# Two tiles of output rows projected one batch later, and the last tile's halves in two PSUM tiles

## The chip, the core and the metric

The kernel runs on one core of a Trainium2 chip. The metric is the device time of one execution in microseconds; the median of several executions is given. A profiled execution has a span, from the first to the last instruction of the core, and a time of its own, which is a little longer.

## The reference

The program is a cross attention over 16 batches. Every batch has 100 query rows of 640 elements, and a context of 722 rows of 384 elements, the last 4 of which are handled apart.

```python
enc = ctx[:, :718];  ca = ctx[:, 718:]
hs  = mha(x @ Wq, enc @ Wk, enc @ Wv)              # 8 heads of 80
q1  = einsum('btc,th->bch', ca, Wq_ca)[:, indices]  # 100 of 384 rows
h1  = mha(q1, x, x)
hs2 = mha(h1 @ Wq, ca @ Wk_ca, ca @ Wv_ca)          # 4 keys
out = (hs + hs2) @ Wout + b_out + x
```

All is float32. The change touches only the last line: `out` has 1600 rows (16 batches of 100), and they are made in tiles of up to 128 rows that don't stop at the borders of batches.

## The kernel before

**Loop.** After a start that loads and rearranges weights, one Python loop (L1102) writes out 16 iterations, one for each batch `b`. The order of the instructions on every engine is the order in which the code issues them. An iteration `b` runs, on TensorE, in this order:

1. `scores` (L604, tile `s_ps`) of batch `b` against its keys, three groups;
2. `softmax2` (L792, `z_ps`) and `products` (L730, `y_ps`), parts of the small attention;
3. `last.transpose()` (L907, `hst_ps`): the attention output of batch `b - 1` is transposed, and ScalarE copies it into tiles `hsT` of 128 output rows each;
4. the values of batch `b` and the keys of batch `b + 1`, interleaved (`vv.go`, `kk.go`; L425 and L456, tiles `v_ps*` and `k_ps*`), then `last_keys` (L549, `kT_ps`);
5. `last.project()` (L932, `o_ps`): every output tile that became complete with batch `b - 1` is multiplied with `Wout`. This is 5 chunks times 2 column halves, 10 matmuls, each two passes with a weight load each in the trace;
6. in odd iterations, `queries` (L525, `q_ps`) for the next two batches;
7. the attention product `a_ps` (L1283) of batch `b`, 96 small matmuls.

Beside it, VectorE and ScalarE make the softmax, GpSimd the small attention's elementwise work (`scores1`, L765; `values2`, L854) and the sums of the context (`enc_sums`, L491), and loads for batch `b + 2` are issued near step 5: `enc`, `mb`, `rest`, `ca` and every other time `xT` from the sync engine's queue (SP), `vb` (1 MB) from GpSimd's.

**Output tiles.** `OC` (L33) lists the row tiles: eleven of 128 rows, one of 64 (rows 1408 to 1471) and the last of 128. A tile is complete with the batch that holds its last row: batches 1, 2, 3, 5, 6, 7, 8, 10, 11, 12, 14, 14 and 15. It is projected in the iteration after. So iterations 1, 5, 10 and 14 project no tile. The 64 rows go through `project_few` in iteration 15, the last tile after the loop.

**Class `Last`** (L873) does this for one batch. `load` (L881) loads the rows of `x` for the tile into `xn` from SP, and GpSimd adds the bias (L892). `project` (L925) takes a `pair`, a PSUM tile of two banks, one bank for each column half; there are two such pairs, shared with the scores and the values. VectorE adds `xn` (L951), and SP stores it (L952). `xn` and `hsT` have two buffers each. For the last batch (`split`) the addition and the store are made for each half apart (L945, L948), and the matmuls come in three calls: chunk 0 of both halves, chunk 1 of both halves, then chunks 2 to 4 of the first half and chunks 2 to 4 of the second.

Of the kernel before, what the change touches and what calls it, by code (L numbers as in the profile page):

```python
# [10 lines left out]
ALU = mybir.AluOpType  # L11
# [3 lines left out]
B, S, H = 16, 100, 640  # L15
# [15 lines left out]


OC = [(r, P) for r in range(0, B * S - P - 64, P)] + [(B * S - P - 64, 64), (B * S - P, P)]  # L33
HT = NH * T

QC = [(0, 64), (64, S)]
# [10 lines left out]
for h in range(NH):  # L47
    lo = h * D
    while lo < (h + 1) * D:
# [3 lines left out]
        lo = hi  # L53
# [71 lines left out]
def kernel(  # L125
# [18 lines left out]
    nc = tc.nc  # L144
# [14 lines left out]
    def pair(name):  # L159
        tile = ps2.tile([P, 2, 512], F32, tag="ps2", name=name)  # L160
        return tile

    def bank(name):
        return pair(name)[:, 0]
# [21 lines left out]
    def hs_tile(name):  # L186
        return main.tile([P, H], F32, tag="hs", name=name)

    def hsT_tile(name):
        return main.tile([P, HC, P], F32, tag="hsT", name=name, bufs=2)  # L190

    def xn_tile(name):
        return main.tile([P, H], F32, tag="xn", name=name, bufs=2)
# [120 lines left out]

    m2 = const.tile([P, HC, NG, HT], F32, name="m2")
    nc.gpsimd.memset(m2, 0.0)
# [8 lines left out]
    for c in range(HC):  # L325
# [13 lines left out]

    m_sb = [t[:, : B * HT] for t in (hs_tile("m_0"), xn_tile("m_1"), xn_tile("m_2"))]  # L340
    m_sb += [
        hsT_tile(f"m_{c}").rearrange("p c s -> p (c s)")[:, : B * HT] for c in range(3, HC)
    ]
    m_d = dram.tile([HC, P, B * HT], F32, name="m_d")

# [7 lines left out]
    for j in range(2):  # L353
        y = const.tile([S, NH, HT + 1], F32, name=f"y_{j}")
        nc.gpsimd.memset(y[:, :, HT:], 1.0)
        ys.append(y)
# [352 lines left out]
    class Second:  # L709
# [98 lines left out]
        def load(self):  # L808
            b = self.b
            self.vb = vb = vb_tile(f"vb_{b}")  # L810
            nc.gpsimd.dma_start(
                out=vb[:S],
                in_=va_d[b * T : (b + 1) * T, :].unsqueeze(0).to_broadcast([S, T, H]),
            )
# [58 lines left out]
    class Last:  # L873
# [7 lines left out]
        def load(self):  # L881

            self.xn = {}
            for r, (lo, n) in enumerate(OC):
                if not self.b * S < lo + n <= (self.b + 1) * S:
                    continue
                xn = self.xn[r] = spare[1] if r == len(OC) - 1 else xn_tile(f"xn_{r}")
                rows = x.rearrange("b s n -> (b s) n")[lo : lo + n]
                for at, cols in self.parts(n):
                    to = xn[at : at + n, : cols.stop - cols.start]  # L890
                    nc.sync.dma_start(out=to, in_=rows[:, cols])
                    nc.gpsimd.tensor_tensor(to, to, bias[at : at + n, cols], ALU.add)  # L892
# [7 lines left out]
        def transpose(self, chunks=[(0, HC)]):  # L900
# [4 lines left out]
            for c0, c1 in chunks:  # L905
                for c in range(c0, c1):
                    nc.tensor.transpose(  # L907
                        t_v[:, c], hs[:S, c * P : (c + 1) * P], ident[:S, :S]
                    )
                for r, (lo, n) in enumerate(OC):  # L910
                    first, end = max(lo, b * S), min(lo + n, (b + 1) * S)
                    if first >= end:
                        continue
                    if r not in hsTs:
                        hsTs[r] = (
                            spare[0].rearrange("p (c s) -> p c s", c=HC)
                            if r == len(OC) - 1
                            else hsT_tile(f"hsT_{r}")
# [6 lines left out]
        def project(self, chunks=range(HC)):  # L925
            for r, xn in self.xn.items():
                lo, n = OC[r]
                if chunks[0] == 0:
                    self.o_ps = pair(f"o_ps_{r}")
                o_ps = self.o_ps  # L930
                for c, k in [(c, k) for k in range(2) for c in chunks]:
                    nc.tensor.matmul(  # L932
                        o_ps[:n, k, : H // 2],
                        hsTs[r][:, c, :n],
                        wout_sb[:, c, k * (H // 2) : (k + 1) * (H // 2)],
                        start=(c == 0),
                        stop=(c == HC - 1),
                    )
                if chunks[-1] < HC - 1:
                    continue  # L940
                o_v = out.rearrange("b s n -> (b s) n")[lo : lo + n]
                if self.split:
                    for k in range(2):
                        cols = slice(k * (H // 2), (k + 1) * (H // 2))
                        nc.vector.tensor_tensor(  # L945
                            xn[:n, cols], o_ps[:n, k, : H // 2], xn[:n, cols], ALU.add
                        )
                        nc.sync.dma_start(out=o_v[:, cols], in_=xn[:n, cols])  # L948
                    continue
                both = xn[:n].rearrange("p (k d) -> p k d", k=2)  # L950
                nc.vector.tensor_tensor(both, o_ps[:n, :, : H // 2], both, ALU.add)  # L951
                nc.sync.dma_start(out=o_v, in_=xn[:n])  # L952

        def project_few(self, r):
            lo, n = OC[r]
            xn = self.xn.pop(r)
            o_ps = psumk(f"o_ps_{r}")
            for c in range(HC):
                for at, cols in self.parts(n):
                    nc.tensor.matmul(  # L960
                        o_ps[at : at + n, : H // 2],
                        hsTs[r][:, c, :n],
                        wout_sb[:, c, cols],
                        start=(c == 0),
                        stop=(c == HC - 1),
                    )
            nc.vector.tensor_tensor(
                xn[:, : H // 2], o_ps[:, : H // 2], xn[:, : H // 2], ALU.add
            )
            o_v = out.rearrange("b s n -> (b s) n")[lo : lo + n]  # L970
            for at, cols in self.parts(n):
                nc.sync.dma_start(out=o_v[:, cols], in_=xn[at : at + n, : H // 2])
# [26 lines left out]
    for n, heads in enumerate(HEADS):  # L999
        cols = len(heads) * B * T  # L1000
# [101 lines left out]
    for b in range(B):  # L1102
# [171 lines left out]
        for g in range(2):  # L1274
# [20 lines left out]
            cols = slice(4 * g * D, 4 * (g + 1) * D)  # L1295
# [66 lines left out]
```

## Time and profile before

| what | value |
|---|---|
| median of 3 executions | 960.67 us (958.2 to 962.56) |
| profiled execution, its own time | 961.78 us |
| its span | 960.1 us |
| mean granted TensorE clock | 0.992 of full |
| one projection of a tile on TensorE (`o_ps` start to next start) | 5.38 us |
| one set of queries (`q_ps` start to `a_ps` start) | 8.55 us |
| one addition of 128 x 640 (L951) | 0.82 us |
| one addition of 128 x 320 (L945) | 0.48 to 0.49 us |
| one bias addition of 128 x 640 (L892) | 1.55 us |

The two rows on the projection and the queries are differences of start times in the timeline of iteration 9 (609.17, 614.55 and 623.10 us). Since the matmuls of one step follow each other without a gap, a difference of starts is what the step costs. In this profile PE stands for TensorE's matmuls and PEld for its weight loads, which overlap; DVE is VectorE, ACT ScalarE, POOL GpSimd and SP the sync engine. A `q` after an engine's name is its instruction sequencer or its DMA queue.

### The profile page before, as it was taken

What the parts mean: (1) busy time and instruction counts of PE and PEld (TensorE: products, weight loads), DVE (VectorE), ACT (ScalarE), POOL (GpSimd) and SP (SyncE); (2) the same over time, 40 slices, a digit from 0 to 9 for tenths busy, and PEclk for the clock granted to TensorE, in tenths of its full rate; (3) what the DMA queues carried; (4) which work ended last, traced back from release to release, by engine and by line L of the source; (5) the groups of instructions that cost most, each with busy time, mean ns of one, the idle gap of its engine ahead of it and who ended that gap; (6) DMA issues with size and microseconds to landing.
All of it is one profiled execution on the core that took longest, in us unless ns stands there. A gap on an engine that the chain in (4) does not pass through costs nothing.

```text
span 960.1 us, 25609 instructions
## 1 busy us (share of the span) xinstructions
PE 942.0 (98%) x11215; PEld 801.9 (84%) x11215; DVE 674.0 (70%) x1083; ACT 361.8 (38%) x598; POOL 620.1 (65%) x570
## 2 busy tenths in 40 slices
PE   9899989999999999999999999999999999999998
PEld 6797869888798798978889787898879879898866
DVE  1647686695937869496874959559694796928883
ACT  1233433434324443342434334243432444314341
POOL 4646888485955768487663958638595476845713
PEclk9999999999999999999999999999999999999999
DMA  8912105021040301204040040401204031120100
GB/s 259 293 55 69 34 17 161 3 72 58 4 146 2 94 23 51 87 1 129 1 139 12 1 129 1 135 3 44 72 1 149 2 93 37 44 86 1 59 8 29
DMA packets 45255, 62.48 MB, mean 65 GB/s; under 512 B 13336, under 2 KB 37208, under 8 KB 43544
## 3 DMA queue, kind: packets, MB, share of 16 engines
q1 hardware_dynamic: 41608, 42.97, 15.1%
q0 software_dynamic: 2512, 16.72, 6.0%
q8 instruction: 88, 1.44, 0.6%
q10 hardware_dynamic: 1024, 1.15, 0.4%
q14 instruction: 23, 0.19, 0.1%
HBM read 55.26 MB, written 5.57 MB: 63 GB/s over the span
## 4 chain that ended last, share of the span: by engine, by line
PE 91%; DMA 3%; POOL 2%; DVE 1%; issue 1%; SPq 0%; ACT 0%; ACTq 0%; DVEq 0%; POOLq 0%
PE s_ps L604 11%; PE a_ps L1283 11%; PE v_psA L425 10%; PE v_psB L425 8%; PE k_psA L456 7%; PE kT_ps L549 7%; PE q_ps L525 7%; PE o_ps L932 7%; PE k_psB L456 6%; PE v_psC L425 3%; PE k_psC L456 2%; PE v_psE L425 2%; PE v_psD L425 2%; PE y_ps L730 2%; PE k_psE L456 1%; DMA wout_sb<-in_wqt 1%
## 5 line engine op out<-in xcount | busy, mean ns | idle before, releaser
L765 POOL TENSOR_TENSOR e<-ca,g 100x800 f32<-100x800 f32 x64 | 99.3, 1561 | 142.4 <-DVE most L1136 127.9
L854 POOL TENSOR_TENSOR hs<-vb,p 100x640 f32<-100x640 f32 x64 | 105.7, 1660 | 46.7 <-DVE p L840 38.8
L861 POOL TENSOR_TENSOR hs<-hs,hs 100x640 f32<-100x640 f32 x48 | 113.8, 2372 | 3.8
L1283 PEld LDWEIGHTS a_ps<-vs,st 120*64 120x64 f32 (+3 forms) x3072 | 109.0, 125 | 5.6 <-issue 5.2
L1283 PE MATMUL a_ps<-vs,st 120*64 120x81 f32 (+3 forms) x3072 | 112.0, 234 | 0.0
L425 PE MATMUL v_psA<-wv_sb,enc 128*120 128x320 f32 x360 | 112.0, 434 | 0.0
L1124 DVE TENSOR_TENSOR st<-st,over 120x1600 f32<-120x1600 f32 x48 | 106.9, 2229 | 0.0
L491 POOL TENSOR_TENSOR enc<-enc 128x240 f32<-128x240 f32 x135 | 101.1, 763 | 7.1
L604 PE MATMUL s_ps<-qp,kT 32*120 32x100 f32 x3072 | 99.5, 265 | 1.5 <-issue 1.5
L604 PEld LDWEIGHTS s_ps<-qp,kT 32*120 32x120 f32 x3072 | 96.7, 181 | 3.2 <-issue 1.8
L621 ACT COPY st<-s_ps 120x800 f32<-120x800 f32 x64 | 49.7, 829 | 127.3 <-PE s_ps L604 127.3
L425 PE MATMUL v_psB<-wv_sb,enc 128*120 128x320 f32 x300 | 93.1, 433 | 0.0
L772 POOL TENSOR_TENSOR e<-e,e 100x800 f32<-100x800 f32 x48 | 90.5, 1886 | 3.8
L456 PE MATMUL k_psA<-enc,wk_sb 128*128 128x240 f32 x360 | 88.4, 369 | 4.4 <-POOL enc L491 2.3
L456 PEld LDWEIGHTS k_psA<-enc,wk_sb 128*128 128x128 f32 x360 | 68.4, 191 | 21.9 <-POOL enc L491 2.8
L1294 DVE RECIPROCAL rs<-a_ps 100x4 f32<-100x4 f32 x32 | 5.8, 181 | 114.9 <-PE a_ps L1283 114.9
L425 PEld LDWEIGHTS v_psA<-wv_sb,enc 128*120 128x120 f32 x360 | 64.5, 183 | 23.0 <-issue 0.5
L1132 ACT ACTIVATE st<-st 120x1600 f32<-120x1600 f32 x48 | 73.9, 1539 | 22.5 <-DVE st L1124 22.5
L1136 DVE TENSOR_TENSOR most<-most,st 120x800 f32<-120x800 f32 x64 | 66.0, 1031 | 22.4 <-ACT st L615 21.2
L491 POOL TENSOR_TENSOR enc<-enc,rest 128x240 f32<-128x240 f32 x45 | 31.8, 706 | 74.2 <-DMA rest<-in_enct 27.4
L456 PE MATMUL k_psB<-enc,wk_sb 128*128 128x240 f32 x300 | 74.7, 372 | 0.0
L425 PEld LDWEIGHTS v_psB<-wv_sb,enc 128*120 128x120 f32 x300 | 54.8, 183 | 22.1 <-DVE vs L396 0.4
(137 smaller groups left out, 1764.9 us busy)
## 6 DMA issues: line engine op xcount, KB each, us to landing
vb<-va_d POOLq DMA_DIRECT2D x16, 1000.0 KB, 7.4
enc<-in_enct SPq DMA_DIRECT2D x30, 240.0 KB
enc<-in_enct SPq DMA_DIRECT2D x15, 360.0 KB
xT<-in_xt SPq DMA_DIRECT2D x8, 500.0 KB
rest<-in_enct SPq DMA_DIRECT2D x31, 120.0 KB
xn<-in_x SPq DMA_DIRECT2D x11, 320.0 KB
out<-xn SPq DMA_DIRECT2D x11, 320.0 KB
ca<-in_cas SPq DMA_DIRECT2D x16, 156.2 KB
```

Source lines behind the costliest of these rows:

```text
L425: nc.tensor.matmul(at[0][j][:KN, : H // 2], a_form(self.enc, f)[:, j * KN : (j + 1) * KN], wv_sb[:, W_AT[f]], start=first, stop=last, skip ...
L456: nc.tensor.matmul(at[:, i * KT : (i + 1) * KT], wk_sb[:, W_AT[f], i], a_form(self.enc, f), start=(first and i == 0), stop=last, skip_grou ...
L491: nc.gpsimd.tensor_tensor(out, left, right, op)
L525: nc.tensor.matmul(q_ps[:, : 2 * S].rearrange("p (j s) -> p j s", j=2), wq_sb[:, c, n * P : (n + 1) * P], xT[:, :, c, :], start=(c == 0), ...
L604: nc.tensor.matmul(s_ps[r][:n, 256 * a + lo : 256 * a + hi], kT[rows, c, u, j * KN : (j + 1) * KN], rhs, start=(a == 0 and c == 0), stop=( ...
L765: first = nc.gpsimd.tensor_tensor(to, self.ca[:, t, :].unsqueeze(1).to_broadcast([S, NH, S]), g[:, :, t].unsqueeze(2).to_broadcast([S, NH, ...
L772: nc.gpsimd.tensor_tensor(e, e, to, ALU.add)
L854: first = nc.gpsimd.tensor_tensor(to, vb[:S, t, :].rearrange("p (h d) -> p h d", h=NH), p2[:, :, t].unsqueeze(2).to_broadcast([S, NH, D]), ...
L861: nc.gpsimd.tensor_tensor(sums, sums, to, ALU.add)
L1124: return nc.vector.tensor_tensor(st[i], st[i], top.over[:KN].unsqueeze(1).to_broadcast([KN, 2, ROWS]), ALU.subtract,)
L1132: nc.scalar.activation(st[i], st[i], AF.Exp, scale=SCALE)
L1283: nc.tensor.matmul(a_v[lo:hi, h % 4], st[i // 2][: KEYS[i], i % 2, h * S + lo : h * S + hi], block(i, h // 4)[: KEYS[i], h % 4], start=(i ...
```

## The change

A tile that became complete with an even batch is projected one batch later, if no tile becomes complete with the odd batch after it. That holds for two tiles: rows 768 to 895 (complete with batch 8, projected in iteration 10 instead of 9) and rows 1152 to 1279 (complete with batch 12, projected in iteration 14 instead of 13). Iterations 10 and 14 make no queries. The load of `x`, the bias addition, the addition and the store of these tiles move along, since they go by the same list.

For the last tile, the two column halves of `o_ps` get a PSUM tile each (one bank of a pair each, so both pairs), where they had the two banks of one pair. The order of the matmuls stays.

```diff
 OC = [(r, P) for r in range(0, B * S - P - 64, P)] + [(B * S - P - 64, 64), (B * S - P, P)]
+
+
+ENDS = [(lo + n - 1) // S for lo, n in OC]
+O_AFTER = [b + 1 if b % 2 == 0 and b + 1 not in ENDS else b for b in ENDS]
 HT = NH * T
...
             for r, (lo, n) in enumerate(OC):
-                if not self.b * S < lo + n <= (self.b + 1) * S:
+                if self.b != O_AFTER[r]:
                     continue
...
-                if chunks[0] == 0:
-                    self.o_ps = pair(f"o_ps_{r}")
+                if chunks[0] == 0 and self.split:
+                    self.o_ps = [bank(f"o_ps_{r}_{k}") for k in range(2)]
+                elif chunks[0] == 0:
+                    self.o_both = pair(f"o_ps_{r}")
+                    self.o_ps = [self.o_both[:, k] for k in range(2)]
                 o_ps = self.o_ps
                 for c, k in [(c, k) for k in range(2) for c in chunks]:
                     nc.tensor.matmul(
-                        o_ps[:n, k, : H // 2],
+                        o_ps[k][:n, : H // 2],
...
-                            xn[:n, cols], o_ps[:n, k, : H // 2], xn[:n, cols], ALU.add
+                            xn[:n, cols], o_ps[k][:n, : H // 2], xn[:n, cols], ALU.add
...
-                nc.vector.tensor_tensor(both, o_ps[:n, :, : H // 2], both, ALU.add)
+                nc.vector.tensor_tensor(
+                    both, self.o_both[:n, :, : H // 2], both, ALU.add
+                )
```

## The prediction

> **What bounds the kernel now.** I read the page first, then its chain of waits, then the TensorE waits, then the timeline and the windows of single iterations.
>
> ```profile
> PE 942.0 (98%) x11215; PEld 801.9 (84%) x11215; DVE 674.0 (70%) x1083; ACT 361.8 (38%) x598; POOL 620.1 (65%) x570
> PE 91%; DMA 3%; POOL 2%; DVE 1%; issue 1%; SPq 0%; ACT 0%; ACTq 0%; DVEq 0%; POOLq 0%
> q8 instruction: 88, 1.44, 0.6%
> ```
>
> TensorE is busy for 942 of 960.1 us and 91% of the chain that ended last is its own. The change removes no matmul, so only idle or slowed TensorE time can be won. The third line is the queue that fetches instructions, 88 packets, used below. In the list of TensorE's waits only one entry lies inside the steady loop and has no releaser:
>
> ```profile
> PE s_ps L604 <- issue: 1.5, 1, 1.5
> ```
>
> The others above 0.5 us belong to the start and to iterations 0 and 1. The windows cut from one z_ps start to the next give the length of an iteration (columns: length, then busy us and count of PE, PEld, DVE, ACT, POOL, then granted clock, DMA share, GB/s):
>
> ```profile
> 405.17:458.97 53.80, 53.80 (x673) 45.30 (x670) 41.79 (x67) 21.48 (x34) 38.52 (x34) 1.00 0.20 58
> 348.30:405.17 56.87, 56.87 (x703) 50.01 (x700) 40.71 (x66) 23.35 (x39) 36.85 (x33) 1.00 0.20 58
> 575.02:637.28 62.26, 62.26 (x724) 53.80 (x720) 41.31 (x67) 23.41 (x40) 38.14 (x34) 1.00 0.19 53
> 637.28:689.07 51.79, 50.30 (x654) 43.31 (x650) 41.06 (x66) 21.41 (x33) 37.46 (x33) 0.97 0.20 54
> ```
>
> They are iterations 6, 5, 9 and 10. Iteration 5 makes queries and projects nothing; 6 projects one tile and makes no queries; 9 does both; 10 does neither. Pair 5+6 holds the same kinds of matmul as pair 9+10, one projection and one set of queries, yet takes 56.87 + 53.80 = 110.67 us against 62.26 + 51.79 = 114.05 us. The 3.38 us are all in iteration 10, the only one of the four whose PE busy is below its length and whose clock is below 1. There the timeline shows where:
>
> ```profile
> 671.51 6.97 PE L1283 MATMUL a_ps<-vs,st 120*64 120x81 f32 x192
> 678.41 0.47 PE L604 MATMUL s_ps<-qp,kT 32*120 32x100 f32 x8
> 680.37 0.78 PE L604 MATMUL s_ps<-qp,kT 32*120 32x100 f32 x21 [1.49 <-issue]
> ```
>
> and the windows show what surrounds it:
>
> ```profile
> 672.00:675.00 3.00, 3.00 (x92) 3.00 (x88) 2.89 (x6) 0.44 (x2) 1.40 (x5) 1.00 0.84 232
> 675.00:678.00 3.00, 3.00 (x92) 3.00 (x89) 2.33 (x5) 0.87 (x1) 0.00 (x0) 1.00 0.96 260
> 678.00:681.00 3.00, 1.51 (x47) 1.34 (x44) 1.54 (x3) 0.00 (x0) 2.58 (x4) 1.00 0.23 72
> 681.00:684.00 3.00, 3.00 (x76) 3.00 (x72) 0.00 (x0) 0.33 (x1) 2.84 (x5) 0.63 0.02 5
> ```
>
> My reading: TensorE ran out of instructions. From 671.51 it starts 92 + 88 = 180 instructions per 3 us. 22,430 matmuls and weight loads over 88 fetches is about 255 instructions a fetch, so a fetch lasts 255/60 = 4.3 us here. Meanwhile the DMA engines are full with the loads for iteration 12, vb's 1 MB among them. Split by queue, 658 to 677.9 us held none of queue 8, only these two; 677.9 to 682 held two fetches:
>
> ```profile
> q1 hardware_dynamic: 1983, 1.43, 26.0%
> q0 software_dynamic: 128, 1.02, 19.5%
> ...
> q8 instruction: 2, 0.03, 2.9%
> ```
>
> In iteration 8, which projects and has the same kind of burst, the seven us after a_ps began at 560.85 held two fetches and TensorE had no wait. So a fetch came late, cost 1.49 us, and the clock then stood below full, which slowed the scores: s_ps to z_ps took 689.07 - 678.41 = 10.66 us, against 575.02 - 567.75 = 7.27 us after iteration 8, again 3.39 us.
>
> [...]
>
> **The change part by part.** Only two tiles move: rows 768 to 895 from iteration 9 to 10, rows 1152 to 1279 from 13 to 14.
>
> *Matmuls.* Each move takes 10 matmuls, 20 passes and 20 weight loads in the trace, 5.38 us (o_ps 609.17, q_ps 614.55), out of an odd iteration and into an even one. The sum is nil. But iteration 9 becomes a copy of 5, and 10 a copy of 6: a_ps of 10 begins 5.4 us later against its own loads, when vb has landed (671 to 676.8 before), and o_ps runs in the burst at 13 + 12 instructions per 3 us[...]. Gain: 114.05 - 110.67 = 3.38 us. Bounds: 0 if another stall takes its place; 1.49 if the same stall usually occurs without the clock drop; 3.38 as profiled. I take 3.38.
>
> *Iterations 13 and 14* are 62.26 and 48.40 us, sum 110.66, already what 5+6 take: nothing to win, except a wait of 0.37 us before the last z_ps matmul at 916.9, also without a releaser. It may go when vb is over before a_ps; between 0 and 0.37, I take 0.
>
> *DVE.* One addition of 0.82 us (L951) moves beside each projection. In 10 it stands after the e subtraction that ends at 676.28, and before a reciprocal whose a_ps half would then end near 680.5; o_ps ends near 677, the addition near 677.9. Cost nil; in iteration 6 the same order shows no TensorE wait. If that cover went, at most 0.82 us twice.
>
> *POOL.* The bias addition (L892, 1.55 us) moves in front of the first hs product (L854), which waits 2.19 us for DVE in iterations 10 and 14. It fits in that wait; bound 0 to 1.55 us of POOL time, no TensorE time.
>
> *SP.* In 10 the xn load of row tile 7, issued at 672.5 before, and the ca load go behind the output of the moved tile, which waits for its addition near 678. That takes 0.48 MB out of the burst and puts it with 0.32 MB of output after it, as in iteration 6 (output at 445.81, then xn, ca). In 14 the three xn loads, before issued at 846 to 849, and the spare load (897.24) go behind the output near 908. They land some microseconds later; the bias additions then run near 912 to 916 instead of 901 to 906, and the first reader, DVE at 923.9, still has about 8 us. Cost nil, 0.5 us at worst. Late release of a hsT or xn buffer: its next writer is an iteration off. Nil.
>
> *The last tile's two PSUM tiles.* The matmul order stays. Before, one addition waits for all of o_ps and the second follows it:
>
> ```profile
> 951.64 4.50 PE L932 MATMUL o_ps<-wout_sb,spare 128*128 128x320 f32 x16
> 956.17 0.89 DVE L945 TENSOR_TENSOR spare<-o_ps,spare 128x320 f32<-128x320 f32 x2 [4.90 <-PE o_ps L932]
> ...
> 956.74 0.82 SPq L948 DMA_DIRECT2D out<-spare  x2
> ```
>
> With two tiles the first half's addition can run after its own last matmul, six passes (6 x 0.27 = 1.6 us) earlier, and its transfer too. After the last matmul there is then one addition and one issue: 0.82/2 = 0.41 us less. [...] Bounds 0.2 to 0.6, I take 0.41. The added waits cost nothing visible, since the second PSUM tile's former user ended near 943.3.
>
> *Sum.* The profiled execution took 961.78 us, 960.1 of span and 1.68 around it. 961.78 - 3.38 - 0.41 = 957.99. It stands 1.11 us above the median of the runs shown, 960.67; the same subtraction from the median gives 956.88. Part of the 1.11 may be the clock drop itself[...]. I go halfway: 957.4.
>
> **The rivals.**
>
> *A, forecast:* the stall goes and nothing replaces it: 957.4, its own range 956.0 to 959.5 (the gap alone, 1.49 + 0.41 off the median, gives 958.8). For it: five even iterations with a projection, none with a stall. Chance 0.62.
>
> *B, the stall moves:* in 14, the output and the loads behind it now fall in the first 5 us of a_ps, and a fetch due there waits as one did in 10. It saves 0.41 and returns 3.38: about 960.3 from the median. Against it: iteration 6 has out, xn and ca there (0.8 MB), without a wait. Chance 0.12.
>
> *C, more than counted:* the 0.37 us goes too, and the executions of before have had other clock drops or such gaps, as their spread of 4.4 us allows. One more half-clock stretch of 3.4 us saved is 1.7: 956.88 - 0.37 - 1.7 = 954.8. Against it: nothing in the start is touched. Chance 0.21.
>
> *D, slower:* [...] In 9 and 13 a_ps begins 5.4 us earlier, at 617.7 and 847.8, and in 14 it meets the deferred loads. If all three stall at 3.38 and only one goes: 960.67 + 2 x 3.38 - 0.41 = 967.0. [...] Against it: iteration 5, the copy of 9, ended its burst as a_ps began (391) without a wait. Chance 0.05.
>
> **How the numbers follow.** About 0.5% (4.8 us, below 955.9 or above 965.5) is what a measurement of this kernel can tell from no change. Faster: C's 0.21 and 0.06 of A. Same: 0.56 of A, B and 0.01 of D. Slower: 0.04 of D. The range 955.0 to 960.9 holds A, B and part of C.
>
> **What would show it.** Right: iteration 10 near 53.8 us with clock 1.00, 9 near 56.9, no wait at s_ps, fetches in the middle of a_ps; one addition after the last matmul. Wrong: a wait without a releaser in 9, 13 or 14, a clock below 1 there, or TensorE waiting for xn, hs or enc.

## The result, and the profile after

| | before | changed |
|---|---|---|
| median of 10 executions | 960.2 us (958.2 to 962.56) | 956.79 us (955.12 to 958.27) |
| profiled execution, own time | 961.78 us | 958.27 us |
| its span | 960.1 us | 956.6 us |
| mean granted clock | 0.992 | 0.993 |

The ratio is 0.9964, with a 95% interval of 0.9952 to 0.9975: 3.4 us less. The interval lies wholly below 1, so the decrease stands clear of the noise, though it is under the 0.5% that the prediction took as the least that can be told from no change.

The windows of iterations 9, 10, 13 and 14 of the changed kernel, cut from one z_ps start to the next as before (length; busy us and count of PE, PEld, DVE, ACT, POOL; granted clock, DMA share, GB/s):

```profile
575.89:632.76 56.87, 56.87 (x703) 50.00 (x699) 40.93 (x66) 23.41 (x40) 36.84 (x33) 1.00 0.20 58
632.76:686.61 53.85, 53.85 (x674) 45.35 (x670) 41.76 (x67) 21.41 (x33) 38.37 (x34) 1.00 0.20 58
802.65:859.53 56.88, 56.88 (x704) 50.00 (x700) 40.64 (x66) 23.41 (x40) 36.90 (x33) 1.00 0.16 46
859.53:913.33 53.80, 53.80 (x674) 45.31 (x670) 43.12 (x67) 21.41 (x33) 32.81 (x20) 1.00 0.14 42
```

In all four TensorE's busy time is the whole length and the clock is full. Pair 9+10 fell from 114.05 to 110.72 us. Pair 13+14 sums to 110.68 us, and was 110.66 before. The list of TensorE's waits has lost both entries without a releaser that it had before: 1.5 us at `s_ps` in iteration 10, and 0.4 us at `z_ps` in iteration 15. What is left belongs to the start and to iterations 0 and 1; its longest lines:

```profile
PE w_ps L1046 <- DMA kT<-in_wkt: 3.5, 1, 3.5
PE k_psA L460 <- POOL enc L495: 2.3, 1, 2.3
PE k_psA L460 <- DVE kT L400: 2.2, 1, 2.2
PE v_psD L429 <- DVE z L807: 1.6, 1, 1.6
```

The place in iteration 10, from the timeline, now with a projection ahead of the attention product and no wait in the scores:

```profile
666.96 5.55 PE L939 MATMUL o_ps<-wout_sb,hsT 128*128 128x320 f32 x20
672.43 6.97 PE L1292 MATMUL a_ps<-vs,st 120*64 120x81 f32 x192
679.33 1.10 PE L608 MATMUL s_ps<-qp,kT 32*120 32x100 f32 x32
```

And the end of the kernel, from the timeline of all engines:

```profile
948.69 4.50 PE L939 MATMUL o_ps<-wout_sb,spare 128*128 128x320 f32 x16
...
951.61 0.49 DVE L952 TENSOR_TENSOR spare<-o_ps,spare 128x320 f32<-128x320 f32 x1 [3.29 <-PE o_ps L939]
952.18 1.90 SPq L955 DMA_DIRECT2D out<-spare  x2
953.23 0.49 DVE L952 TENSOR_TENSOR spare<-o_ps,spare 128x320 f32<-128x320 f32 x1 [1.12 <-PE o_ps L939]
```

The first half's addition runs 1.62 us ahead of the second's, while the other half's matmuls go on. Only one addition stands behind the last matmul. From the last transposes to the end it is 8.18 us, and was 8.75.

The two profiled spans differ by 3.5 us. By place: pair 9+10 brings -3.3, iteration 15 up to the last transposes -0.5 (35.56 to 35.05 us, the 0.37 us wait before the last z_ps matmul among it), the end -0.6, iteration 3 -0.1, and the stretch up to the third z_ps start +1.0 (178.32 to 179.32 us). That last one is in code that the change leaves alone, and shows how far two executions differ there: in the first 140 us the clock of the changed kernel's profile stood at half for 13.7 us, that of the profile before for 10.2 us.

### The profile page after: what moved, and what is told of

The parts are those of the page before. It is cut to its first block, busy times and chain, and to the rows that moved or that the text cites. A ratio compares the mean times of both kernels' runs of the same rounds, so it can differ in the third digit from the quotient of the medians.

```text
span 956.6 us, 25607 instructions
## 1 busy us (share of the span) xinstructions
PE 940.4 (98%) x11215; PEld 800.2 (84%) x11215; DVE 674.9 (71%) x1083; ACT 361.6 (38%) x598; POOL 621.5 (65%) x570
## 3 DMA queue, kind: packets, MB, share of 16 engines
q8 instruction: 88, 1.44, 0.6%
## 4 chain that ended last, share of the span: by engine, by line
PE 91%; DMA 3%; POOL 2%; DVE 1%; issue 1%; SPq 0%; ACT 0%; ACTq 0%; POOLq 0%
PE s_ps L608 11%; PE a_ps L1292 11%; PE v_psA L429 10%; PE v_psB L429 8%; PE k_psA L460 7%; PE kT_ps L553 7%; PE q_ps L529 7%; PE o_ps L939 7%; PE k_psB L460 6%; PE v_psC L429 3%; PE k_psC L460 2%; PE v_psE L429 2%; PE v_psD L429 2%; PE y_ps L734 2%; DMA kT<-in_wkt 1%; PE k_psE L460 1%
## 5 line engine op out<-in xcount | busy, mean ns | idle before, releaser
L608 PE MATMUL s_ps<-qp,kT 32*120 32x100 f32 x3072 | 97.4, 263 | 0.0
L608 PEld LDWEIGHTS s_ps<-qp,kT 32*120 32x120 f32 x3072 | 94.7, 179 | 1.6 <-issue 0.2
```

What stands on the lines that cost most here:

```text
L608: nc.tensor.matmul(s_ps[r][:n, 256 * a + lo : 256 * a + hi], kT[rows, c, u, j * KN : (j + 1) * KN], rhs, start=(a == 0 and c == 0), stop=( ...
```

## The experiments

All times are medians, with the ratio to the kernel before as it ran beside each. The first four runs had a median of 959.93 us beside them, the last three 959.31 us.

**1. The move alone.** The kernel before with the new list and the new condition in `load`, and the last tile in one pair.

```diff
+ENDS = [(lo + n - 1) // S for lo, n in OC]
+O_AFTER = [b + 1 if b % 2 == 0 and b + 1 not in ENDS else b for b in ENDS]
...
-                if not self.b * S < lo + n <= (self.b + 1) * S:
+                if self.b != O_AFTER[r]:
```

> Only the two row tiles are projected later; the last tile keeps one pair. Theory (a late instruction fetch in iteration 10 is the gain): iteration 10 takes 53.8 us and 9 takes 56.9, no wait in the scores, and the time is 0.4 to 0.6 us above the full change, about 957.3. Rival (the last tile's two PSUM tiles are most of the gain): 959.5 or more.

Measured: 957.6 us, ratio 0.9977 (0.9967 to 0.9988). Iterations 9 and 10 took 56.87 and 53.80 us, and no TensorE wait is in the scores. The move is most of the gain, about 2.2 us (1.2 to 3.2 by the interval).

**2. The split alone.** The changed kernel with every tile projected where it was.

```diff
-O_AFTER = [b + 1 if b % 2 == 0 and b + 1 not in ENDS else b for b in ENDS]
+O_AFTER = ENDS
```

> Only the last tile's halves get two PSUM tiles; all tiles are projected where they were. Theory: the end, from the last transposes on, is 0.4 to 0.6 us shorter; iteration 10 keeps its wait in the scores (iteration near 51.8 us, or 50 without the clock drop); about 959.7. Rival (the split is most of the gain): 957.5 or less.

Measured: 959.78 us, ratio 0.9994 (0.9984 to 1.0005). In the trace the end is 8.19 us, as in the full change, so 0.56 us shorter. The executions can't tell that from nothing, but the traces can: over all nine profiles of this study the end takes 8.18 to 8.19 us in the three with two PSUM tiles and 8.67 to 8.76 us in the six with one pair. Iteration 10 is as it was, in the windows and in the waits:

```profile
637.61:689.61 52.00, 50.31 (x654) 43.32 (x650) 40.52 (x66) 21.40 (x33) 36.65 (x33) 0.97 0.20 54
```
```profile
PE s_ps L608 <- issue: 1.7, 1, 1.7
```

Also here iteration 15 takes 35.01 us to the last transposes. So the 0.37 us wait that it had in the profile of before is not taken away by the move of the second tile. In the other eight profiles iteration 15 takes 35.00 to 35.27 us, with either list of tiles.

**3. The suspected transfer taken out of the way, no projection moved.** In iteration 10 alone, `vb` (1 MB) is loaded behind the context sums.

```diff
-            second.load()
+            if b != 10:
+                second.load()
...
             enc_sums(enc_next)
+            if b == 10:
+                second.load()
```

> The kernel before with one thing changed: in iteration 10 alone the 1 MB load of vb is issued behind the context sums, some 16 us later, so that it isn't in the burst in which a_ps begins. No projection moves. Theory (vb's transfer holds up TensorE's instruction fetch): the wait without a releaser goes, iteration 10 takes 53.8 - 5.4 = 48.4 us at clock 1.00, a fetch lands within the first 5 us of a_ps, and the time falls by about 3, to 957.3. Rival (the scores wait for a result of another engine or for a PSUM buffer, and the projection gives cover): iteration 10 stays near 51.8 us and the time at 960.2.

Measured: 958.09 us, ratio 0.998 (0.9972 to 0.9988). Windows of iterations 9 and 10:

```profile
576.29:638.54 62.25, 62.25 (x723) 53.80 (x719) 41.30 (x67) 23.39 (x40) 38.11 (x34) 1.00 0.18 53
638.54:686.95 48.41, 48.41 (x653) 41.50 (x649) 41.79 (x66) 21.40 (x33) 38.14 (x33) 1.00 0.13 36
```

The time fell by 1.8 us (1.2 to 2.7 by the interval), where about 3 was expected. Iteration 10 does the same work as before in 48.41 us, TensorE is busy throughout and the clock is full. VectorE and ScalarE have nothing done sooner by the edit: the subtraction of `e` starts 3.8 us after `a_ps` both times. GpSimd has: its context sums start 2.86 us after `a_ps` here and 6.83 us before. The scores don't read them, and experiment 4 shows that an early start of the sums is no cure: there they start after 0.97 us, and the wait in iteration 10 is 2.34 us. The attention product began at 672.78 here. The packets by queue from 672.7 to 680.1 us have one instruction fetch, and none of `q0`, the queue that carried `vb`:

```profile
q1 hardware_dynamic: 1083, 0.81, 38.8%
q8 instruction: 1, 0.02, 1.2%
```

Narrower windows put that fetch at 676.15. This is the direct test of the cause: the rival expected iteration 10 near 51.8 us, and it falls.

**4. The transfer put into the way, in six iterations.** The changed kernel, where in iterations 2, 4, 6, 8, 10 and 12 the load of `vb` waits for the projection's last matmul, so that it runs in the first microseconds of a_ps.

```diff
-            second.load()
+            if b % 2 or b == B - 2:
+                second.load()
...
             keys(m_next)
+            if b % 2 == 0:
+                second.load(last.done)
             enc_sums(enc_next)
...
-            nc.gpsimd.dma_start(
+            dma = nc.gpsimd.dma_start(
...
+            if behind:
+                wait_for(dma, behind)
...
-                    nc.tensor.matmul(
+                    self.done = nc.tensor.matmul(
```

> The changed kernel with the load of vb held back in iterations 2, 4, 6, 8, 10 and 12 until the projection's last matmul, so that its transfer falls into the first 6 us of a_ps. Theory: fetches due there are late, waits without a releaser come back in a_ps or the scores of several of these iterations, 0.5 to 3 us each, with clock drops behind some; the time rises by 5 to 20 us over the changed kernel. Rival (a transfer doesn't hold up TensorE; the wait in iteration 10 had another cause): within 1.5 us of the changed kernel.

Measured: 967.56 us, the median of four executions, ratio 1.0082 (1.0066 to 1.0098). That is 10.8 us above the changed kernel's median, which was measured at another time; by the two ratios it is 11.3 us. The windows of the six iterations, 53.80 us each where nothing is late:

```profile
177.84:231.88 54.04, 54.04 (x674) 45.50 (x670) 41.74 (x67) 21.46 (x34) 38.51 (x34) 1.00 0.20 58
294.13:348.94 54.81, 54.14 (x674) 45.58 (x670) 41.82 (x67) 21.46 (x34) 38.50 (x34) 1.00 0.18 51
405.81:460.90 55.09, 54.12 (x673) 45.47 (x669) 41.91 (x67) 21.46 (x34) 38.51 (x34) 1.00 0.20 57
523.15:577.25 54.10, 54.10 (x673) 45.58 (x669) 41.81 (x67) 21.46 (x34) 38.52 (x34) 1.00 0.18 52
634.13:692.32 58.19, 55.85 (x673) 47.19 (x669) 41.76 (x67) 21.40 (x33) 38.50 (x34) 0.97 0.19 53
754.57:811.97 57.40, 55.88 (x674) 47.22 (x670) 41.80 (x67) 21.49 (x35) 38.51 (x34) 0.97 0.17 49
```

The six lengths stand 10.8 us above six times 53.80. Four have a wait without a releaser:

```profile
PE s_ps L608 <- issue: 5.5, 4, 2.3
```

These are iterations 4, 6, 10 and 12, with 0.67, 0.97, 2.34 and 1.52 us. Iterations 2 and 8 have no wait and are still 0.24 and 0.30 us longer, which stays unexplained. The odd iterations, where the load was not touched, stay at 62.25 and 56.87 us. This transfer can make the wait: it did so in four of the six iterations.

**5. Each of the two moves by itself**, on the kernel of experiment 1. The diff is that of the second tile; the first has 8 in the place of 12.

```diff
-O_AFTER = [b + 1 if b % 2 == 0 and b + 1 not in ENDS else b for b in ENDS]
+O_AFTER = [b + 1 if b == 12 else b for b in ENDS]
```

> The kernel before with only rows 1152 to 1279 projected later (iteration 14 instead of 13). Theory (a move gains only where it parts a_ps from the loads of its iteration, and iteration 14 loads little): iteration 10 keeps its wait, 13 takes 56.9 us and 14 takes 53.8, their sum as before, and the time stays at 959.9 within 0.7. Rival (an even iteration without projection loses time as such, so each move brings its half): about 958.5.

> The kernel before with only rows 768 to 895 projected later (iteration 10 instead of 9). Theory: all of the gain of the two moves, 957.6 within 0.7. Rival (each move brings its half): about 958.8.

Measured: the second tile 959.99 us, ratio 1.0011 (1.0001 to 1.0021); the first 957.49 us, 0.9978 (0.9970 to 0.9986). The first move is all of the gain. The second brings none: its interval is a loss of 0.1 to 2.0 us, and in its profile iterations 13 and 14 together take 110.67 us, where they took 110.66. In its profile iterations 10, 13 and 14 are:

```profile
637.56:687.51 49.95, 48.68 (x653) 41.68 (x650) 41.33 (x66) 21.40 (x33) 36.39 (x32) 1.00 0.20 56
803.72:860.60 56.88, 56.88 (x704) 50.01 (x700) 41.33 (x66) 23.40 (x40) 36.88 (x33) 1.00 0.17 47
860.60:914.39 53.79, 53.79 (x673) 45.30 (x669) 41.29 (x67) 21.40 (x33) 33.23 (x20) 1.00 0.14 42
```

The first line tells more than the median does. The wait is there, 1.27 us, but the clock stayed full, and the iteration lost only 49.95 - 48.41 = 1.54 us, where it lost 3.38 with a clock drop.

Iteration 14 of the kernel before is a control that was there from the start. It has no projection either, and `vb` moved from 0.3 to 4.5 us after its `a_ps` began, yet it has no wait. Its fetch began to move at 4.5 us, with 226 instructions still to run before it was needed (the count is explained below), so nothing was late there that a move could cure.

**6. The same bytes from another queue.** The kernel before, where in iteration 10 alone `vb` is loaded from ScalarE's queue, behind the copies of the last keys.

```diff
-        def load(self):
+        def load(self, engine=nc.gpsimd):
...
-            nc.gpsimd.dma_start(
+            engine.dma_start(
...
-            second.load()
+            if b != 10:
+                second.load()
...
             last_keys(b + 1, enc)
+            if b == 10:
+                second.load(nc.scalar)
```

> The kernel before with the 1 MB load of vb of iteration 10 alone issued from ScalarE's queue instead of GpSimd's, behind the copies of the last keys, about 1 us later; bytes and addresses are the same. Theory a (it is the bytes ahead of the fetch on the shared engines): the wait in the scores stays, 1 to 3 us, iteration 10 stays at 51.5 us or more, the time at 959.5 or more. Theory b (it is GpSimd's software queue): no wait, iteration 10 at 48.4 us, the time near 958.

Measured: 959.12 us, ratio 1.0009 (0.9996 to 1.0022), the executions spread from 957.2 to 963.46. Iteration 10 and its wait:

```profile
637.42:686.76 49.34, 48.78 (x654) 41.75 (x650) 40.42 (x66) 21.40 (x33) 32.76 (x27) 1.00 0.21 57
```
```profile
PE s_ps L604 <- issue: 0.6, 1, 0.6
```

Neither theory holds as stated: the wait is there, so it isn't GpSimd's queue alone, but it is 0.56 us, not 1 to 3. The load also began to move 1.3 us later against `a_ps`, and took 6.6 us, where it had taken 5.2. The packets show one more thing. In the four profiles with a wait in iteration 10 and `vb` on GpSimd's queue, the fetch began to move 0.3 to 1.0 us after `vb`'s last packet had landed; here it began 2.9 us before that. So a fetch did pass in the middle of such a transfer. From GpSimd's queue it did so too, in iterations 2 and 6 of experiment 4, but only in the last microsecond. How much is bytes, how much the queue's kind, stays open.

**All fetches together.** In these nine profiles TensorE has the same instructions from the start of iteration 10's attention product on, and the 61st fetch of queue 8 is the one due there. Narrow windows of the DMA view give when it began to move; the gap is the idle time in the timeline.

```
kernel            a_ps starts   fetch moves   after a_ps   gap    fetch - gap
first tile           670.59        673.55        2.96        0
move alone           670.96        673.93        2.97        0
vb late              672.78        676.15        3.37        0
full change          672.43        676.93        4.50        0
vb from ACT          671.69        676.90        5.21       0.56       4.65
second tile          671.80        677.84        6.04       1.27       4.77
before               671.51        677.98        6.47       1.49       4.98
split alone          671.85        678.50        6.65       1.69       4.96
vb behind o_ps       673.83        681.06        7.23       2.34       4.89
```

Up to 4.5 us after the start a fetch cost nothing. The last column puts the limit at 4.65 to 4.98 us; beyond it each microsecond of delay is about a microsecond of idle TensorE. This holds for this place of this kernel. The full change stands close to the limit: its fetch moved at 4.50 us, though `vb` had landed before `a_ps` began, where the same move alone had it at 2.97 us. What held it up is not resolved.

**Where TensorE stops.** The traces allow a test that needs no timing. Number all instructions of TensorE in the order in which they start: 11,215 weight loads, 11,215 matmuls and 173 others, 22,603 in the profile of before. In the five profiles with a wait in iteration 10, TensorE stops each time behind number 15,809. The three other waits of experiment 4 stand behind numbers 7,617, 10,433 and 18,625. All these numbers differ by whole multiples of 256, about as many as one fetch holds (22,603 instructions over the 88 packets of queue 8, 1.44 MB in all, are about 257 each). The 0.37 us wait of iteration 15 stands behind number 21,953, which is in the same row. In all nine cases TensorE goes on 2.4 to 2.7 us after a fetch began to move, whether the wait was 0.37 or 2.34 us.

So all nine are waits for the next 256 instructions, the small one in iteration 15 too. From 130 us on, no profile has another idle stretch of TensorE over 0.1 us before the final additions. The count also says how late the fetch was: in the profile of before a fetch begins to move when 242 instructions (the median) are left before the place where TensorE would stop without it. For the fetch in iteration 10 it was 31. In the profile of the changed kernel it was 145, and 209 in that of experiment 3.

## Why the prediction was right

The forecast was 957.4 us, and 956.79 came out.

- *The late fetch.* Right. Experiment 3 removes the wait without moving a projection, experiment 4 makes it in four iterations, the table shows how the wait grows with the delay, and the count shows that every wait stands at the end of a block of 256. In the changed kernel `vb`'s last packet landed 0.26 us before `a_ps` of iteration 10 began, as the prediction had it. That a load can delay a fetch is what experiments 3 and 4 show: with `vb` out of the way the fetch moves 3.37 us after the start of `a_ps`, where it was 6.47, and with `vb` put into the way 7.23, where it was 4.50. With a projection in the burst, TensorE starts 13 matmuls and 12 weight loads per 3 us there (667 to 670 us of the changed kernel, DMA share 0.98) against 92 and 88 in `a_ps`; from these counts I estimate that 256 instructions last about 31 us at the one rate and 4.3 us at the other.
- *Iterations 9 and 10 become copies of 5 and 6.* Right: 56.87 and 53.85 us against 56.87 and 53.80.
- *The gain of 3.38 us.* Right for the profiled execution (3.33), too large for the usual one. The move alone is 1 - 0.9977 = 2.2 us, its interval 1.2 to 3.2; the first tile alone 2.1. The smaller case that the prediction had named, the wait without the clock drop, is in the profile of the second tile, 1.54 us. The granted clocks of the executions hint that it is the more frequent: the mean clock is 0.993 or less in 17 of the 77 executions of the kernel before that ran beside the experiments, and in 2 of the 30 of the two kernels without the wait (move alone, first tile alone). It is only a hint, since half-clock stretches at the start vary as well (10.2 and 13.7 us in the two profiles). The sum for a profiled execution was 957.99 us, and the profiled execution of the changed kernel took 958.27. The step from there halfway to the median was a guess; it took back 0.6 us of the 1.2 us by which 3.38 was too large. That the forecast came within 0.6 us of the median owes something to luck.
- *Iterations 13 and 14 give nothing.* Right: 110.68 against 110.66 us, and experiment 5.
- *The 0.37 us before the last z_ps matmul, taken at 0.* It went, but not by the move of the second tile: it is absent in experiment 2 too. It was a late fetch as well, as the count shows; four other profiles have 0.07 to 0.08 us at the same instruction, four have none.
- *DVE, POOL and SP at nil.* Right as far as the traces show: no new TensorE wait for xn, hs, enc or a PSUM buffer appeared. The bias additions of iteration 15 did wait for their loads, and ended near 909, some 12 us before the first reader.
- *The end, taken at 0.41 us.* The traces show 0.57 and 0.56. The addition gives 0.41 as worked out. The further 0.16 us lies behind the last addition: from its start to the end of the span 3.33 us, before 3.50 (956.58, 0.41 after the first, to 960.08). What shortened it was not shown.
- *Rivals.* B did not come: iteration 14 has no wait. C did not come as a whole: the 0.37 us went, but the start was not faster. The half-clock stretch in its sum is as long as the trace has it: at 681.80 us of the profile of before the clock stands at 0.50 for 3.413 us. D's stall can be made, as experiment 4 shows (0.67 to 2.34 us), but in 9, 13 and 14 the change doesn't bring transfer and attention product together: `vb`'s last packet landed 3.25, 3.01 and 0.80 us before `a_ps` began.

The measured 3.4 us stands above the 2.2 of the move and the 0.6 of the end together; the intervals reach about 1 us to either side, so nothing more has to be explained.

## What to carry to other kernels

An idle stretch on TensorE without a releaser, in a phase of many small matmuls and under a burst of loads, is a candidate for a late instruction fetch: look whether a fetch is missing in the packets of the burst, and compare with an iteration that has the same work without the gap. With several such stretches, count TensorE's instructions up to each: here they lay whole multiples of 256 apart. Here two things cured it: a projection between burst and dense phase, with fewer and longer matmuls (20 in 5.55 us against 192 in 6.97), and one load of 1 MB moved out of the way (experiment 3). Price such a stall from several executions: iteration 10 lost 3.38 us with a clock drop behind the wait and 1.54 us without, and the wait itself differs from one profile to the next (1.27, 1.49 and 1.69 us with the same code at that place).

## What the runs showed that I had not expected

- A gap on TensorE of 1.5 to 2.3 us was followed by a stretch at half clock in some places (3.413 us at 0.50 in the profile of before), and in others not. Behind the gaps of 1.49, 1.69, 2.34 and 1.52 us of the late fetches the clock dropped, behind that of 1.27 us it did not. But in the profile of before a gap of 1.55 us in iteration 1 (from 119.97 us) has full clock behind it too, until 125.42 us, when a second gap of 2.26 us has passed. So the length of one gap does not decide it. In that profile the four half-clock stretches ahead of the final additions begin at 33.27, 84.47, 125.42 and 681.80 us and last 3.413 us each, and the last three begin 15, 27 and 190 times 3.413 us behind the first. In the profile of the changed kernel two stretches of 6.827 us, twice that length, begin at 31.91 and 124.07 us, 27 times 3.413 us apart. What decides whether one comes was not shown.
- The drop was worth about as much as the wait ahead of it: beyond the wait itself iteration 10 lost 3.38 - 1.49 = 1.89 us with a drop, and 1.54 - 1.27 = 0.27 us without, so by my estimate from these the drop took about 1.6 us.
- An instruction fetch of 16.4 KB (1.44 MB over 88) took 0.9 to 1.8 us to move in the profile of before, and yet one load of 1 MB held it up for microseconds. In iteration 10 it began to move 6.0 to 7.2 us after `a_ps` in the four profiles with `vb` from GpSimd's queue in the way, and after 3.0 to 4.5 us in the four where `vb` had landed by 0.8 us after `a_ps` began, or came later.
